# Stores of finished rows and loads of residual rows emitted when they are due, and a shorter assumed trip through DRAM

## The chip, the cores and the metric

The kernel runs on one core of one Trainium2 chip. The metric is the device time of one execution in microseconds (us); each figure is a median over runs.

## The reference

One transformer block with adaptive layer norm, in 32-bit floats, on x of shape (8, 1024, 512) with a condition vector of 512 for each of the 8 sequences:

```
mod = silu(condition) @ Wada + bada
sh_a, sc_a, gt_a, sh_m, sc_m, gt_m = split(mod, 6)
xm = layernorm(x, g1, be1) * (1 + sc_a) + sh_a
x  = x + gt_a * attention(xm, Wqkv, Wproj, bproj)      # 16 heads of 32, causal
xm = layernorm(x, g2, be2) * (1 + sc_m) + sh_m
h  = gelu(xm @ W1 + b1)                                # 512 -> 2048, exact gelu
x  = x + gt_m * (h @ W2 + b2)
```

## The kernel before

**Blocks.** The 8 sequences are cut into 16 blocks of 512 rows (`blocks`, numbered `n`; `NB` is 16). A block holds four tiles of 128 rows. For each block the kernel makes k, q and v, the attention, the projection with the first residual addition (`project_out`, the step "proj"), the second norm ("mt"), the four steps "u" of the up projection with gelu, and the four parts "d" of the down projection. The products k, q, v and up are done by a Strassen scheme (`strassen`) of seven block products named A11, S2, A12, S1, S3, S4, A22 in the order in which TensorE does them; each takes one 256 KB piece of weights. The down projection uses the same scheme in another order.

**Two streams and a planner.** While one block's attention runs, the dense steps of its neighbours run beside it. The order is made once, when the program is built: dense work is written as Python generators (threads) that yield the keys they need. `now` holds a modelled clock for each engine, `written` and `left` hold the modelled times at which a key is written and free again. `work` advances the thread with the shortest modelled wait, side threads ahead of the main one when waits are equal, and what a thread emits goes at once to the ends of the engines' queues. The engines then run those queues strictly in order. So a modelled time decides only where an instruction stands in its queue; on the chip semaphores decide when it runs. The list of dense steps (`plan`) is fixed; at a border between blocks it reads: rest of "u" and "d" of block n-1, "v" of block n+1, "load_xr" of block n, "proj" of n, "mt" of n, "k" of n+2.

**Banks.** Dense products go to three PSUM banks. A bank is free again when VectorE (DVE) or ScalarE (ACT) has copied or combined it out. Inside `strassen`, A11 is copied out to a partial `p1` (traced as `p_v` for v); S2 is combined with it on DVE (`u_v`); A12 is added into A11's bank, which is copied out as the first quarter of the result and freed; S1 takes the third bank and is combined on DVE; S3 needs a bank again; S4 and A22 come last in a side thread.

**The DMA queue.** All loads and stores in question are issued by SyncE (SP), in order; a DMA whose inputs aren't ready holds all that are queued behind it. The weights come through a ring of nine pieces (`fetch`): a load is emitted when the piece nine places earlier is released. Wproj's four pieces stand in this ring between v's and the next k's.

**Residual rows.** `residual[n]` is a tile `xr` of 1 MB in a pool of one buffer (another pool for block 14). "load_xr" (L1268) issues four loads of 256 KB for block n, which must wait until block n-1's rows have been stored. `store(n, t)` (L1104) issues two stores of 256 KB for a pair of tiles; it is called in the last part of "d" right after `settle` has emitted the additions to these rows, most of them on GpSimd (POOL). Both are emitted at the place of the call.

**The trip through DRAM.** For blocks 2 to 15 the normalized rows are transposed without TensorE (`turn`): four DVE transposes of 32x32 blocks, a store of 1 MB to a DRAM tile (`held_a<-xm_a`, L673), four loads of 256 KB back in another order (`hat_a<-held_a`, L678). After each leg `turn` yields until a key is due that the model puts `HOLDING` = 8000 ns after the emission. Then `modulated` emits, one after the other, the instructions that read the loaded tile: four scalings on ACT (L738) or DVE (L732), and subtractions that make the operands T1 to T4 (L746, L748, L158). They are needed only for a later block's k, q and v.

Of the kernel before, what the change touches and what calls it, by code (L numbers as in the profile page):

```python
# [9 lines left out]
F32 = mybir.dt.float32  # L10
# [12 lines left out]
def kernel(  # L23
# [33 lines left out]
    nc = tc.nc  # L57
    B, T, D = x.shape
    HD = W1.shape[1]
    P = 128  # L60
    hd = D // H
    scale = float(hd) ** -0.5
    TB = 512
    NTT = TB // P
# [11 lines left out]
    kvp = ctx.enter_context(tc.tile_pool(name="kvp", bufs=3))  # L76
    act = ctx.enter_context(tc.tile_pool(name="act", bufs=2))
    xrp = ctx.enter_context(tc.tile_pool(name="xrp", bufs=1))
# [11 lines left out]
    blocks = [(b, h) for b in range(B) for h in range(NHALF)]  # L90
    NB = len(blocks)


    now = {"PE": 0.0, "DVE": 0.0, "ACT": 0.0, "POOL": 0.0}
    written, left = {}, {}
    shape = [None]
    pool_spans = []
    NEVER = float("inf")
# [5 lines left out]
    def due(reads=(), writes=()):  # L104
        t = 0.0
        for k in reads:
            t = max(t, written.get(k, 0.0))
        for k in writes:
            t = max(t, left.get(k, 0.0))
        return t  # L110
# [128 lines left out]
    for w in range(1, NB):  # L239
        n = w - 1  # L240
# [27 lines left out]
    n = NB - 1  # L268
# [76 lines left out]
    def take(count):  # L345
        i = taken[0]
        taken[0] += count
        return list(range(i, taken[0]))
# [18 lines left out]
    rows = tmp.tile([P, TB], F32, tag="y", name="rows")[:n_rows, :P]  # L367
    at, r0 = [], 0
# [85 lines left out]
    def half(i, size):  # L454
        return slice(i * size, (i + 1) * size)
# [200 lines left out]
    def turn(key, rows, xm):  # L656
# [16 lines left out]
        nc.sync.dma_start(held, small_blocks)  # L673
        written["held", key] = now["PE"] + HOLDING
        yield [("held", key)], []
        for m in range(NTT):
            some = held[:, ts(m, D)].rearrange("(a i) d -> i a d", i=Q)
            nc.sync.dma_start(rows[ts(m, Q), :, :], some)  # L678
        written["turned", key] = now["PE"] + HOLDING
        yield [("turned", key)], []  # L680

    HOLDING = 8000
    turns = [0]

    def modulated(key, gain, shift, b, guards):
# [68 lines left out]
    def accumulate(pairs, reads=(), close=True):  # L754
        yield reads, [BANK]
        bank = lin_bank()
        for i, (lhsT, rhs) in enumerate(pairs):
            if i:
                yield [], []
            matmul(banks[bank], lhsT, rhs, i == 0, close and i == len(pairs) - 1, reads, bank)  # L760
        return bank
# [227 lines left out]
        yield [("v moved", n)], []  # L989
        vs[n] = v  # L990

    residual, stored = {}, {}
    y_count, y_keys = [0], {}

    def y_key(kind, new=False):
# [5 lines left out]
    LANDING = 10000  # L1001

    def add_to(xt, other, reads, writes, op=ALU.add):
        either(xt, xt, other, op, [*reads, *writes], writes)

    def project_out(n):
        at = take(NC)
        yield [("attended", n)], []
        attT = qTs[n]
        tiles = [residual[n][:, t, :] for t in range(NTT)]  # L1010
        for t, xt in enumerate(tiles):
            xt_job = lambda t=t, xt=xt: add_to(xt, gate_rows["gba"], [("row", "gba")], [("xr", n, t)])
            pool_jobs.append((xt_job, [("xr", n, t)]))
        last = n == NB - 1
        begun = []

        def begin(t):

            bank = yield from accumulate(
                [(attT[:, c, ts(t, P)], piece(at[c])) for c in range(NC - 1)], [("att", n)], False  # L1020
            )
            begun.append(bank)

        for t, xt in enumerate(tiles):
            if last:
                while len(begun) <= max(t, 1):
                    yield from begin(len(begun))
                bank = begun[t]
                yield [("att", n, t)], []
                matmul(  # L1030
                    banks[bank], attT[:, NC - 1, ts(t, P)], piece(at[NC - 1]), False, True,
                    [("att", n, t)], bank,
                )
            else:
                bank = yield from accumulate(
                    [(attT[:, c, ts(t, P)], piece(at[c])) for c in range(NC)], [("att", n)]
                )
            y = tmp.tile([P, D], F32, tag="y", name=f"y_{n}_{t}", bufs=2)
            ky = y_key("proj", True)
            combine_out(y, bank, banks[bank], gate_rows["ga"], [("row", "ga")], [ky], ALU.mult)  # L1040
            if last:
                run_pool_jobs(True)
                nc.vector.tensor_tensor(xt, xt, y, ALU.add)
                note("DVE", 700, [ky, ("xr", n, t)], [("xr", n, t)], port=True)
                following = normalize_tile(xt, f"m{n}", t, ("xr", n, t))
                if t > 0:
                    pending()
                pending = following
            else:
                add_to(xt, y, [ky], [("xr", n, t)])  # L1050
        if last:
            pending()
        release(*at)
        run_pool_jobs(True)
        if not last:
            normalize(residual[n], f"m{n}", [("xr", n, t) for t in range(NTT)])
# [35 lines left out]
    def settle(n, f, t, y, ky):  # L1092
# [4 lines left out]
        add_to(y, gate, [("row", "gm")], [ky], ALU.mult)  # L1097
        add_to(residual[n][:, half(t, 2), c], y, [ky], keys)

    def store(n, t):  # L1100
        b, h = blocks[n]
        for i in (2 * t, 2 * t + 1):
            r0 = h * TB + i * P
            nc.sync.dma_start(out[b, r0 : r0 + P, :], residual[n][:, i, :])  # L1104
        stored[n + 1] = max(stored.get(n + 1, 0.0), due([("xr", n, 2 * t), ("xr", n, 2 * t + 1)]))

    def down(n, part):

# [136 lines left out]
    def perform(step):  # L1245
        kind = step[0]
        if kind == "mod":
            yield from modulation(step[1])
        elif kind == "norm_columns_a":
            columns_of["a"] = norm_columns("a", 0, 1, O_G1, O_BE1)  # L1250
        elif kind == "gates":
            yield from gates(step[1])
        elif kind == "columns_m":
            columns_of["m"] = norm_columns("m", 3, 4, O_G2, O_BE2)
        elif kind == "load_xa":
            x_pre[step[1]] = load_x(step[1])
            written["x", f"a{step[1]}"] = now["PE"] + 6000
        elif kind == "load_xr":
            n = step[1]
            b, h = blocks[n]  # L1260
            if n == NB - 2:
                xr = kvp.tile([P, NTT, D], F32, tag="kT", name=f"xr_{n}")
            else:
                xr = xrp.tile([P, NTT, D], F32, tag="xr", name=f"xr_{n}")
            residual[n] = xr
            for t in range(NTT):
                r0 = h * TB + t * P
                nc.sync.dma_start(xr[:, t, :], x[b, r0 : r0 + P, :])  # L1268
                landed = max(now["PE"], stored.get(n, 0.0)) + LANDING + 700 * t
                written["xr", n, t] = landed  # L1270
        elif kind == "norm_a":
            key = f"a{step[1]}"
            normalize(x_pre.pop(step[1]), key, [("x", key)] * NTT)
        elif kind == "at":
            n = step[1]
            guards = [("m used", n - 3)] if n > 2 else [("v done", 0)] if n == 2 else []
            start(modulated(f"a{n}", *columns_of["a"], blocks[n][0], guards))
        elif kind == "beside":
            start(perform(step[1]))
        elif kind == "sums":  # L1280
            sum_weights(step[1:])
        elif kind == "mt":
            n = step[1]
            guards = [("v done", n + 1)]
            start(modulated(f"m{n}", *columns_of["m"], blocks[n][0], guards))
        elif kind == "k":
            if step[1] != 3:
                yield [("free for k", step[1])], []
            yield from project_T(step, kTs, kvp, "kT", lambda: None)
        elif kind == "q":  # L1290
            yield from project_T(step, qTs, act, "qT", lambda: projected.add(step[1]))
        elif kind == "v":
            yield from project_v(step)
        elif kind == "preps":
            prepared[0] = [preparation(), 0.0]
            written["prepared up"] = written["prepared"] = NEVER
        elif kind == "rows":
            gate_broadcasts(*step[1:])
        elif kind == "proj":
            yield from project_out(step[1])  # L1300
        elif kind == "u":
            yield from up(step)
        elif kind == "d":
            yield from down(*step[1:])
# [19 lines left out]
    def start(it):  # L1324
        thread = [it, None]
        sides.append(thread)
        advance(thread)
# [509 lines left out]
    for n in range(NB):  # L1837
        written["attended", n] = NEVER
        written["v done", n] = NEVER
        written["m used", n] = NEVER  # L1840
        if n > 1:
            written["free for v", n] = NEVER
        if n > 2:
            written["free for k", n] = NEVER
# [70 lines left out]
```

## Time and profile before

| | us |
|---|---|
| median of 3 runs | 3562.32 (3561.42 to 3562.63) |
| profiled execution, its own time | 3568.64 |
| span in that profile | 3566.9 |
| TensorE (PE) busy in it | 3490.9 |
| VectorE (DVE) busy | 2181.1 |
| GpSimd (POOL) busy | 2081.8 |
| ScalarE (ACT) busy | 1186.3 |

The granted TensorE clock was 0.995 over the span. The 2 us between the span and the profiled execution's own time lie outside the first and the last instruction. "SPq" marks an instruction of the DMA queue of SyncE; the name after an arrow in a wait is what ended the wait. A timeline row gives the start, the length, the engine, the line, the operation, the tiles, the number of merged instructions and, in brackets, the idle time before it and who ended it.

### The profile page before, as it was taken

What the parts mean: (1) busy time and instruction counts of PE and PEld (TensorE: products, weight loads), DVE (VectorE), ACT (ScalarE), POOL (GpSimd) and SP (SyncE); (2) the same over time, 40 slices, a digit from 0 to 9 for tenths busy, and PEclk for the clock granted to TensorE, in tenths of its full rate; (3) what the DMA queues carried; (4) which work ended last, traced back from release to release, by engine and by line L of the source; (5) the groups of instructions that cost most, each with busy time, mean ns of one, the idle gap of its engine ahead of it and who ended that gap; (6) DMA issues with size and microseconds to landing.
All of it is one profiled execution on the core that took longest, in us unless ns stands there. A gap on an engine that the chain in (4) does not pass through costs nothing.

```text
span 3566.9 us, 120690 instructions
## 1 busy us (share of the span) xinstructions
PE 3490.9 (98%) x54621; PEld 1741.5 (49%) x54621; DVE 2181.1 (61%) x2395; ACT 1186.3 (33%) x1229; POOL 2081.8 (58%) x2247
## 2 busy tenths in 40 slices
PE   8999999999999999999999999999999999999999
PEld 4444445444554545445454454544545445454445
DVE  6776575665746557365574665746666466665663
ACT  2334333352323514234241442323423134231521
POOL 3667746675456754577536675366762667526660
PEclk9999999999999999999999999999999999999999
DMA  6753434435453344533445334453344533434334
GB/s 201 241 179 93 141 102 127 124 108 155 113 150 107 104 154 117 158 100 101 146 121 148 105 102 146 120 151 103 103 140 126 152 103 105 143 108 142 92 111 137
DMA packets 318259, 461.77 MB, mean 129 GB/s; under 512 B 27052, under 2 KB 177388, under 8 KB 315700
## 3 DMA queue, kind: packets, MB, share of 16 engines
q1 hardware_dynamic: 317632, 454.03, 43.4%
q8 instruction: 430, 7.05, 0.8%
q14 instruction: 81, 0.66, 0.1%
q10 hardware_dynamic: 116, 0.03, 0.0%
HBM read 408.80 MB, written 43.06 MB: 127 GB/s over the span
## 4 chain that ended last, share of the span: by engine, by line
PE 88%; DMA 4%; POOL 3%; DVE 3%; ACT 1%; issue 1%; SPq 1%; ACTq 0%; DVEq 0%; POOLq 0%
PE bank L202 60%; PE sc L1517 8%; PE po L1650 7%; PE st L1610 7%; PE st L1598 3%; DMA w<-in_L_cond_Wproj_dram 2%; PE bank L1671 2%; POOL pT L1740 1%; DMA hat_a<-held_a 1%; PE bank L728 1%; DVE mx L1534 1%; POOL hT L161 1%; PE bank L1572 0%; DVE sc L1531 0%; DMA w<-in_L_cond_Wada_dram 0%
## 5 line engine op out<-in xcount | busy, mean ns | idle before, releaser
L1740 POOL TENSOR_TENSOR pT<-pT,pT 128x256 f32<-128x256 f32 (+3 forms) x1254 | 1213.2, 1003 | 336.1 <-PE po L1650 183.4
L1622 ACT ACTIVATE pT<-st 128x2048 f32<-128x2048 f32 x288 | 541.0, 1878 | 1115.0 <-PE st L1610 1032.9
L202 PE MATMUL bank<-w,hT 128*32 128x256 f32 x14336 | 813.7, 380 | 0.2 <-POOL pT L1627 0.2
L1534 DVE TENSOR_REDUCE mx<-sc 128x4 f32<-128x2048 f32 (+3 forms) x384 | 666.0, 1755 | 216.2 <-PE sc L1517 210.0
L202 PEld LDWEIGHTS bank<-w,hT 128*32 128x32 f32 x14336 | 451.6, 110 | 367.6 <-issue 82.5
L202 PE MATMUL bank<-xm_m,w 128*32 128x256 f32 x8192 | 498.4, 380 | 0.0
L202 PE MATMUL bank<-t_m,w 128*32 128x256 f32 x6144 | 383.2, 380 | 0.1
L202 PEld LDWEIGHTS bank<-xm_m,w 128*32 128x32 f32 x8192 | 256.0, 110 | 222.2 <-issue 55.5
L1627 POOL TENSOR_SCALAR_AFFINE_SELECT pT<-pT 128x512 f32<-128x512 f32 x256 | 169.0, 678 | 332.4 <-ACT pT L1622 332.2
L1517 PE MATMUL sc<-kT,qT 32*128 32x512 f32 (+3 forms) x3072 | 329.1, 520 | 2.0 <-DVE mx L1534 1.7
L1531 DVE TENSOR_TENSOR sc<-sc,mask 128x1024 f32<-128x1024 f32 (+1 forms) x160 | 162.8, 1018 | 273.5 <-PE sc L1517 187.3
L1650 PE MATMUL po<-pT,v 128*32 128x512 f32 (+3 forms) x3048 | 303.1, 493 | 2.0 <-POOL pT L1627 2.0
L1610 PE MATMUL st<-qT,kT 32*128 32x512 f32 (+3 forms) x3072 | 300.6, 487 | 0.0
L202 PEld LDWEIGHTS bank<-t_m,w 128*32 128x32 f32 x6144 | 189.4, 110 | 180.7 <-issue 57.5
L202 PE MATMUL bank<-w,qT 128*32 128x512 f32 x2048 | 244.7, 606 | 21.2 <-DMA w<-in_L_cond_Wproj_dram 19.7
L1689 DVE RECIPROCAL rec<-rec 128x128 f32<-128x128 f32 x256 | 224.5, 919 | 33.2 <-ACT rec L1680 33.2
L202 PE MATMUL bank<-xm_a,w 128*32 128x256 f32 x3968 | 244.6, 380 | 0.0
L1517 PEld LDWEIGHTS sc<-kT,qT 32*128 32x128 f32 x3072 | 129.3, 183 | 172.8 <-ACT pT L1622 63.9
L202 PE MATMUL bank<-t_a,w 128*32 128x256 f32 x2944 | 190.9, 382 | 0.4 <-ACT xm_m L738 0.4
L193 DVE TENSOR_TENSOR hT<-bank,u_u 128x512 f32<-128x512 f32 x192 | 129.3, 685 | 101.2 <-PE bank L202 99.9
L1064 ACT ACTIVATE hT<-hT,cols 128x512 f32<-128x512 f32 x256 | 164.5, 711 | 55.3 <-DVE hT L193 54.7
L202 PEld LDWEIGHTS bank<-xm_a,w 128*32 128x32 f32 x3968 | 123.5, 110 | 106.5 <-issue 30.8
(216 smaller groups left out, 3396.6 us busy)
## 6 DMA issues: line engine op xcount, KB each, us to landing
w<-in_L_cond_W_dram SPq DMA_DIRECT2D x384, 256.0 KB
w<-kept_up_S SPq DMA_DIRECT2D x256, 256.0 KB
w<-kept_down_S SPq DMA_DIRECT2D x256, 256.0 KB
w<-kept_qkv_S SPq DMA_DIRECT2D x180, 256.0 KB
w<-in_L_cond_Wqkv_dram SPq DMA_DIRECT2D x147, 256.0 KB
hat_a<-in_x_dram SPq DMA_DIRECT2D x64, 256.0 KB
w<-in_L_cond_Wproj_dram SPq DMA_DIRECT2D x64, 256.0 KB
xr<-in_x_dram SPq DMA_DIRECT2D x64, 256.0 KB
```

The costliest lines, as they stand in the source:

```text
L193: nc.vector.tensor_tensor(out, src, other, op)
L202: nc.tensor.matmul(ps[r, :], columns, rhs, start=start, stop=stop, skip_group_check=True)
L1064: nc.scalar.activation(hT[:, i, :], hT[:, i, :], AF.Gelu, bias=cols[:, O_B1 + f : O_B1 + f + 1])
L1517: nc.tensor.matmul(sc[:, j, c0 : c0 + w], qTs[n][r, gg, ts(qt, P)], keys_of(n, kh)[r, gg, :w], start=True, stop=True, skip_group_check=True,)
L1531: nc.vector.tensor_tensor(place, place, shape_of.to_broadcast(place.shape), ALU.add)
L1534: nc.vector.tensor_reduce(maxima[n, gg][:, kh, qt, :], sc[:, :, c0 : c0 + w], axis=AX.X, op=ALU.max)
L1610: nc.tensor.matmul(st[:, j, c0 : c0 + w], kT[r, gg, ts(k % NTT, P)], qT[r, gg, TB - w :], start=False, stop=True, skip_group_check=True,)
L1622: nc.scalar.activation(pT[:, :, :used], st[:, :, :used], AF.Exp, scale=scale)
L1627: nc.gpsimd.affine_select(diagonal, diagonal, pattern=[[0, HPG], [1, P]], compare_op=ALU.is_ge, fill=0.0, base=0, channel_multiplier=-1,)
L1650: nc.tensor.matmul(po[r, TB - w :], v[:, k % NTT, g * P + j * hd : g * P + (j + 1) * hd], pT[:, j, c0 : c0 + w], start=(k == 0), stop=last ...
L1689: nc.vector.reciprocal(some, some)
L1740: nc.gpsimd.tensor_tensor(into, into, pT[:, j, c0 : c0 + w], ALU.add)
```

## The change

`store` no longer issues its DMA. It starts a side thread that yields until the additions to the pair of tiles are due by the model, and then emits one DMA of 512 KB in place of two of 256 KB. When both pairs of a block are emitted, the key "stored" of that block is set 3000 ns later (`STORING`). "load_xr" starts a side thread `load_xr(n)`, which yields until "stored" of the block that used the buffer before is due (block 14, in the other pool, waits for nothing; block 15 waits for block 13), and then emits two loads of 512 KB in place of four of 256 KB. The rows are modelled as landed 5000 ns after this plus 700 ns for each tile, where they were modelled at 10000 ns (`LANDING`) plus 700 ns after the later of the emission and the additions. `project_out` now also yields until the loads have been emitted (key "xr begun"). `HOLDING`, the modelled length of each leg of the trip through DRAM, goes from 8000 to 5000 ns.

```diff
--- before.py
+++ after.py
@@ -679,7 +679,7 @@
         written["turned", key] = now["PE"] + HOLDING
         yield [("turned", key)], []
 
-    HOLDING = 8000
+    HOLDING = 5000
     turns = [0]
 
     def modulated(key, gain, shift, b, guards):
@@ -989,7 +989,7 @@
         yield [("v moved", n)], []
         vs[n] = v
 
-    residual, stored = {}, {}
+    residual = {}
     y_count, y_keys = [0], {}
 
     def y_key(kind, new=False):
@@ -1005,7 +1005,7 @@
 
     def project_out(n):
         at = take(NC)
-        yield [("attended", n)], []
+        yield [("attended", n), ("xr begun", n)], []
         attT = qTs[n]
         tiles = [residual[n][:, t, :] for t in range(NTT)]
         for t, xt in enumerate(tiles):
@@ -1097,12 +1097,43 @@
         add_to(y, gate, [("row", "gm")], [ky], ALU.mult)
         add_to(residual[n][:, half(t, 2), c], y, [ky], keys)
 
+    unstored = {}
+
     def store(n, t):
+        unstored.setdefault(n, 2)
+
+        def when_added():
+            b, h = blocks[n]
+            keys = [("xr", n, 2 * t), ("xr", n, 2 * t + 1)]
+            yield keys, []
+            rows = out[b, h * TB + 2 * t * P : h * TB + (2 * t + 2) * P, :]
+            nc.sync.dma_start(rows.rearrange("(t p) d -> p t d", p=P), residual[n][:, half(t, 2), :])
+            unstored[n] -= 1
+            if unstored[n] == 0:
+                written["stored", n] = now["PE"] + STORING
+
+        start(when_added())
+
+    STORING = 3000
+
+    def load_xr(n):
+        before = n - 2 if n == NB - 1 else n - 1
+        if before >= 0 and n != NB - 2:
+            yield [("stored", before)], []
         b, h = blocks[n]
-        for i in (2 * t, 2 * t + 1):
-            r0 = h * TB + i * P
-            nc.sync.dma_start(out[b, r0 : r0 + P, :], residual[n][:, i, :])
-        stored[n + 1] = max(stored.get(n + 1, 0.0), due([("xr", n, 2 * t), ("xr", n, 2 * t + 1)]))
+        if n == NB - 2:
+            xr = kvp.tile([P, NTT, D], F32, tag="kT", name=f"xr_{n}")
+        else:
+            xr = xrp.tile([P, NTT, D], F32, tag="xr", name=f"xr_{n}")
+        residual[n] = xr
+        for t in range(2):
+            rows = x[b, h * TB + 2 * t * P : h * TB + (2 * t + 2) * P, :]
+            nc.sync.dma_start(xr[:, half(t, 2), :], rows.rearrange("(t p) d -> p t d", p=P))
+        for t in range(NTT):
+            written["xr", n, t] = now["PE"] + LOADING + 700 * t
+        written["xr begun", n] = 0.0
+
+    LOADING = 5000
 
     def down(n, part):
 
@@ -1256,18 +1287,8 @@
             x_pre[step[1]] = load_x(step[1])
             written["x", f"a{step[1]}"] = now["PE"] + 6000
         elif kind == "load_xr":
-            n = step[1]
-            b, h = blocks[n]
-            if n == NB - 2:
-                xr = kvp.tile([P, NTT, D], F32, tag="kT", name=f"xr_{n}")
-            else:
-                xr = xrp.tile([P, NTT, D], F32, tag="xr", name=f"xr_{n}")
-            residual[n] = xr
-            for t in range(NTT):
-                r0 = h * TB + t * P
-                nc.sync.dma_start(xr[:, t, :], x[b, r0 : r0 + P, :])
-                landed = max(now["PE"], stored.get(n, 0.0)) + LANDING + 700 * t
-                written["xr", n, t] = landed
+            written["xr begun", step[1]] = NEVER
+            start(load_xr(step[1]))
         elif kind == "norm_a":
             key = f"a{step[1]}"
             normalize(x_pre.pop(step[1]), key, [("x", key)] * NTT)
@@ -1838,6 +1859,7 @@
         written["attended", n] = NEVER
         written["v done", n] = NEVER
         written["m used", n] = NEVER
+        written["stored", n] = NEVER
         if n > 1:
             written["free for v", n] = NEVER
         if n > 2:
```

## The prediction

> **What bounds the kernel now.** I read the page first, then TensorE's waits, then the DMA queue's own waits, then the timeline of one border between blocks, engine by engine.
>
> ```profile
> span 3566.9 us, 120690 instructions
> PE 3490.9 (98%) x54621; PEld 1741.5 (49%) x54621; DVE 2181.1 (61%) x2395; ACT 1186.3 (33%) x1229; POOL 2081.8 (58%) x2247
> ...
> PE 88%; DMA 4%; POOL 3%; DVE 3%; ACT 1%; issue 1%; SPq 1%; ACTq 0%; DVEq 0%; POOLq 0%
> ```
>
> TensorE is busy for 3490.9 of 3566.9 us. The change adds and removes no matmul, so all that it can save lies in the other 76 us; what it can cost is new idle time of TensorE. TensorE's waits say which of the 76 us lie near the change:
>
> ```profile
> PE bank L202 <- DMA w<-in_L_cond_Wproj_dram: 19.7, 14, 3.1
> ...
> PE bank L202 <- DVE v L193: 5.2, 3, 2.1
> ...
> PE bank L202 <- ACT xm_a L738: 1.3, 1, 1.3
> ```
>
> Columns: total us, times, longest. TensorE waits 19.7 us for Wproj's pieces, at the projection that begins each block border. The other two rows are at the same places (a combination of v, or a scaling of a tile back from DRAM, came late). Together 26.2 us: this is the most that I let the change win. The queue in which Wproj's loads stand waits too:
>
> ```profile
> SPq L1104 <- POOL xr L161: 80.5, 23, 9.0
> ...
> SPq L1104 <- DVE xr L158: 24.8, 3, 11.2
> ...
> SPq L1268 <- DMA out_dram<-xr: 11.0, 10, 2.3
> ```
>
> SP stands for 105 us at stores whose additions aren't done, and 11 us at residual loads whose buffer isn't stored yet. One border in order of time, first SP:
>
> ```profile
> 2149.78 0.38 SPq L673 DMA_DIRECT2D held_a<-xm_a  x1
> 2151.08 0.32 SPq L340 DMA_DIRECT2D w<-kept_qkv_S  x1
> 2155.89 1.22 SPq L1104 DMA_DIRECT2D out_dram<-xr  x2
> ...
> 2158.18 0.89 SPq L342 DMA_DIRECT2D w<-in_L_cond_Wproj_dram  x2
> 2161.44 0.82 SPq L1104 DMA_DIRECT2D out_dram<-xr  x2
> 2162.31 3.08 SPq L678 DMA_DIRECT2D hat_a<-held_a  x4
> 2165.49 0.85 SPq L342 DMA_DIRECT2D w<-in_L_cond_Wproj_dram  x2
> ...
> 2168.43 3.73 SPq L1268 DMA_DIRECT2D xr<-in_x_dram  x4
> ```
>
> After the weight load at 2151.08 nothing is issued until the first store at 2155.89; the second pair goes at 2161.44, and the way back from DRAM and the last two Wproj pieces stand behind it. TensorE meanwhile:
>
> ```profile
> 2157.74 1.91 PE L202 MATMUL bank<-w,xm_a 128*32 128x256 f32 x32
> 2159.47 1.91 PE L202 MATMUL bank<-w,t_a 128*32 128x256 f32 x32
> 2161.19 3.64 PE L202 MATMUL bank<-w,xm_a 128*32 128x256 f32 x64
> 2164.65 1.91 PE L202 MATMUL bank<-w,t_a 128*32 128x256 f32 x32
> ...
> 2168.10 1.90 PE L202 MATMUL bank<-w,qT 128*32 128x512 f32 x16
> 2171.79 1.92 PE L202 MATMUL bank<-w,qT 128*32 128x512 f32 x16 [1.79 <-DMA w<-in_L_cond_Wproj_dram]
> 2175.69 3.47 PE L202 MATMUL bank<-w,t_a 128*32 128x256 f32 x32 [1.98 <-DVE v L193]
> ```
>
> The rows are v's A11, S2, A12 with S1, S3; then the projection (w,qT), which runs out of weights and waits 1.79 us, then 1.98 us for DVE. ACT and DVE at the same place:
>
> ```profile
> 2159.76 0.59 ACT L188 COPY p_v<-bank 128x512 f32<-128x512 f32 x1 [13.30 <-PE bank L202]
> 2163.17 0.59 ACT L188 COPY v<-bank 128x512 f32<-128x512 f32 x1 [2.82 <-PE bank L202]
> 2171.36 2.22 ACT L738 ACTIVATE xm_a<-hat_a,shifta,gaina 128x512 f32<-128x512 f32 x3 [7.61 <-DMA hat_a<-held_a]
> ...
> 2161.51 0.69 DVE L193 TENSOR_TENSOR u_v<-bank,p_v 128x512 f32<-128x512 f32 x1 [2.83 <-PE bank L202]
> 2164.95 0.69 DVE L193 TENSOR_TENSOR u_v<-bank,u_v 128x512 f32<-128x512 f32 x1 [2.75 <-PE bank L202]
> 2171.36 0.55 DVE L732 TENSOR_SCALAR xm_a<-hat_a,gaina,shifta 128x512 f32<-128x512 f32 x1 [5.72 <-DMA hat_a<-held_a]
> ```
>
> Both engines stand at the scalings that read the tile back from DRAM. These stand in the queues right behind S1's combination (2164.95), when the model is 16 us past the store at 2149.78 (2165.8): model and chip agree, and only the trip is longer than modelled.
>
> **Part one: stores and residual loads.** The store is emitted when its additions are due, so SP no longer stands at 2151 to 2155.9 and before 2161.4. Weight loads then go when TensorE releases a piece, one each 1.72 us (2159.47 to 2161.19), and Wproj's last piece with the release of A12's, at about 2164.6, where it went near 2166. The projection reads that piece for the first time about 2.5 us after it begins at 2168.10. The traffic of the border (1 MB out, 1 MB back, 1 MB stored, 1 MB of residual rows) also gets spread. I take the 26.2 us as gone: the Wproj waits by the earlier issue, the other two because the blocking scalings move away from there (part two). The gain is bounded by 26.2 above and by 0 below. The residual loads follow 3 us after the second store, which is emitted once the addition behind the store of 2161.44 is done: 2164.4. Main ends its part of v with S3 at 2166.4, so "xr begun" holds nobody by 2 us. If that cover goes, the whole main thread (projection, k, q) is queued behind it, at one us for each us. SP issues half as many stores and residual loads, of twice the size; it had time to spare, and the bytes are the same. The earlier additions to xr (5 for 10 us in the model) are work of POOL and DVE, off the path.
>
> **Part two: 5 for 8 us.** The loads back are now emitted 5 us after the store out, the scalings 10 us after it, where they were emitted at 16. When does the data come? The first trip, with no residual store in the way, and one of the last:
>
> ```profile
> 129.23 1.46 SPq L673 DMA_DIRECT2D held_a<-xm_a  x1
> ...
> 134.78 3.43 SPq L678 DMA_DIRECT2D hat_a<-held_a  x4
> ...
> 144.49 2.21 ACT L738 ACTIVATE xm_a<-hat_a,shifta,gaina 128x512 f32<-128x512 f32 x3
> ...
> 3039.27 0.41 SPq L673 DMA_DIRECT2D held_a<-xm_a  x1
> ...
> 3044.94 2.91 SPq L678 DMA_DIRECT2D hat_a<-held_a  x4
> ```
>
> The way out takes 5.55 and 5.67 us or less, the way back 9.71 at most (134.78 to 144.49, where ACT came from other work) and 9.05 (2162.31 to 2171.36). So I put the tile's landing 14.6 to 15.3 us after the store out (call that moment H), while ACT and DVE will stand at it from about H+10.3 (the model moves in steps of 0.43 us). That wait of 4 to 5 us is no longer than today's; but it falls at v's beginning and not at its end. In this border A11 ends at H+9.9 and its copy gets ahead of the scalings. S2's combination (2161.51 is H+11.7) and the copy that frees A12's bank (H+13.4) come behind them. ACT frees that bank after three scalings and the copy, 2.22 + 0.59 = 2.8 us after the tile lands, at H+17.4 to H+18.1. S3 wants a bank at 2164.65, H+14.87. All three banks are taken, so TensorE waits 2.5 to 3.2 us, with nothing else queued. I count six such borders (v begins 8.0 us after H): 6 x 2.85 = 17.1 us.
>
> In three others v begins 9.7 us after H:
>
> ```profile
> 1706.27 0.38 SPq L673 DMA_DIRECT2D held_a<-xm_a  x1
> ...
> 1717.97 0.59 ACT L188 COPY p_v<-bank 128x512 f32<-128x512 f32 x1 [14.59 <-PE bank L202]
> ...
> 1719.40 3.64 PE L202 MATMUL bank<-w,xm_a 128*32 128x256 f32 x64
> ```
>
> Here A11's copy itself (H+11.7) stands behind the scalings. A12 needs it at 1719.40, H+13.1, and gets it at H+17.4 to H+18.1: 4.3 to 5.0 us, three times, 14.0 us. One border lies between these (v at H+11.0): A12 waits for it from H+14.5, 3.2 us. Four trips are left (two at the start, two where the late store had pushed H back): the scalings meet other work of ACT and DVE there, between 0 and 4 us each, and 1 us each is my estimate: 4 us. Sum 38.3 us. It is bounded below by 0 (the tile comes early enough) and above by 59 us (in the six, too, A11's copy falls behind: A12 waits from H+11.4 to H+17.8, 6.4 us each, 38.4 + 14.0 + 3.2 + 4).
>
> **The sum.** 3568.64 us of the profiled execution - 26.2 + 38.3 = 3580.7. The runs shown have a median of 3562.32, 6.3 lower: 3574.4, forecast 3574.
>
> **Rivals.**
> *Faster: the trip gets shorter once the queue is clear.* If the way back took as little as the way out, 5.6 us, the tile would be there at H+11.2 and S3's bank free at H+14.0, before it is wanted; the three borders would lose 0.9 us each. It decides from a trip of 12 us on. For it: the backlog of stores and loads that stands around hat_a at 2161.44 to 2168.43 goes. Against it: the trip at 129.23 had no residual store beside it and took up to 15.3. Time: 3562.3 - 26.2 + 3 = 3539; halfway, 3551. [...]
>
> *No difference.* The two parts cancel to within 7 us, as with a trip of 13.5 us: the six lose 1.5, the three 3.2, the one 1.8, the four 4 in all; 24 against 26. Time 3560.
>
> *Much slower: A11's copy falls behind the scalings in all ten borders.* The margin is only some 0.4 us (H+10.3 against H+9.9). Time 3562.3 - 26.2 + 59 = 3595.
>
> *It doesn't do what it says.* If the model has the additions done too early, the stores are emitted early and SP stands as today; then part one is lost and part two stays: above 3590. Against it: model and chip agreed at 2165.
>
> **How the numbers follow.** About 0.2% (7 us) is what a measurement can tell from no change. Chances: forecast 0.49, faster 0.26, no difference 0.15, the two slower rivals 0.10. Near the forecast the order of all that follows shifts as well, so its own range is 3567 to 3585 and I leave a twentieth of it inside the 7 us. That makes faster 0.26, same 0.20, slower 0.54. The range 3545 to 3591 leaves out the far half of the faster rival and most of the much slower one.
>
> **What would show it.** SP's waits at stores nearly gone; hat_a issued 5 to 6 us after held_a; Wproj gone from TensorE's waits. In their place TensorE waits at v for `p_v` or `v` on ACT, or for `u_v` on DVE, 2.5 to 5 us in most borders, and DVE's and ACT's waits for hat_a move ahead of u_v. Wrong would be: TensorE without a wait inside v (then 3540), or Wproj still late.

## The result, and the profile after

The changed kernel takes 3618.28 us (median; 3610.07 to 3620.9), beside 3562.48 us (3561.42 to 3575.09) for the kernel before: a ratio of 1.0144, interval 1.0117 to 1.0172. It is slower, as forecast (3574), but by 56 us by the medians (51 by the ratio) where 12 were forecast, and past the upper end of the range (3591). The profiled execution took 3618.11 us; that of the kernel before was 6 us over its median, so the views below show 49.5 of the 56 us.

The page of the kernel after, its span, busy times and chain:

```profile
span 3616.4 us, 120606 instructions
PE 3514.0 (97%) x54621; PEld 1743.9 (48%) x54621; DVE 2153.9 (60%) x2366; ACT 1190.7 (33%) x1236; POOL 2093.2 (58%) x2269
PE 83%; DMA 5%; DVE 5%; POOL 4%; ACT 1%; issue 1%; SPq 1%; ACTq 0%; DVEq 0%; POOLq 0%
```

The span is 49.5 us longer. TensorE's idle time grew from 76.0 to 102.4 us, by 26.4. But its busy time grew too, by 23.1 us, with the same 54621 matmuls: idle time is only about half of the loss. TensorE's waits, of the kernel after (total us, times, longest):

```profile
PE bank L202 <- ACT p_v L188: 15.6, 4, 4.3
PE bank L202 <- ACT v L188: 14.5, 6, 2.9
PE po L1671 <- POOL pT L1648: 10.4, 6, 2.0
...
PE bank L202 <- DMA w<-in_L_cond_Wproj_dram: 4.5, 3, 1.9
...
PE bank L202 <- DVE v L193: 1.6, 1, 1.6
```

The first two rows are the forecast waits inside v, in all ten borders: four for A11's copy `p_v`, six for the copy that frees A12's bank. Wproj is down from 19.7 to 4.5 us and `v` on DVE from 5.2 to 1.6; the wait for a scaling, 1.3 us before, has no row in this list for the dense products. The third row is new in size: there the attention's products wait for POOL, 2.0 us in all before, 10.4 now. The DMA queue's own waits after:

```profile
SPq L1110 <- POOL xr L161: 12.3, 10, 3.0
...
SPq L1131 <- DMA out_dram<-xr: 6.2, 2, 3.6
...
SPq L1110 <- DVE xr L158: 5.3, 3, 3.0
```

SP stands at these stores for 17.6 us in place of 105.3 (the last block has its own, which the change leaves as they were). The border that the prediction showed lies 41.4 us later in the kernel after. Its timeline there, first SP, then TensorE, ACT and DVE:

```profile
2191.16 0.68 SPq L673 DMA_DIRECT2D held_a<-xm_a  x1
2196.73 2.86 SPq L678 DMA_DIRECT2D hat_a<-held_a  x4
2199.63 0.43 SPq L342 DMA_DIRECT2D w<-in_L_cond_Wproj_dram  x1
2200.16 0.40 SPq L1110 DMA_DIRECT2D out_dram<-xr  x1
2200.66 1.42 SPq L342 DMA_DIRECT2D w<-in_L_cond_Wproj_dram  x2
2202.80 0.40 SPq L1110 DMA_DIRECT2D out_dram<-xr  x1
2203.29 0.95 SPq L342 DMA_DIRECT2D w<-in_L_cond_Wproj_dram  x1
2211.72 0.90 SPq L1131 DMA_DIRECT2D xr<-in_x_dram  x2
```

```profile
2199.12 1.91 PE L202 MATMUL bank<-w,xm_a 128*32 128x256 f32 x32
2202.57 3.64 PE L202 MATMUL bank<-w,xm_a 128*32 128x256 f32 x64
2208.26 2.99 PE L202 MATMUL bank<-w,t_a 128*32 128x256 f32 x32 [2.06 <-ACT v L188]
2211.00 1.74 PE L202 MATMUL bank<-w,qT 128*32 128x512 f32 x8
```

```profile
2201.14 0.59 ACT L188 COPY p_v<-bank 128x512 f32<-128x512 f32 x1 [13.30 <-PE bank L202]
2205.51 2.23 ACT L738 ACTIVATE xm_a<-hat_a,shifta,gaina 128x512 f32<-128x512 f32 x3 [3.79 <-DMA w<-in_L_cond_Wproj_dram]
2207.64 0.56 ACT L188 COPY v<-bank 128x512 f32<-128x512 f32 x1
...
2205.52 0.55 DVE L732 TENSOR_SCALAR xm_a<-hat_a,gaina,shifta 128x512 f32<-128x512 f32 x1 [5.46 <-DMA w<-in_L_cond_Wproj_dram]
```

With H = 2191.16: `hat_a` is issued at H+5.6, all four Wproj pieces are issued by H+13.1, and the projection (w,qT) starts without a wait. A11's copy is ahead of the scalings (H+10.0). ACT and DVE then stand at the scalings until the tile lands, at H+14.35 (the profile names Wproj's load there; I take it for `hat_a`, the loaded tile that the scalings read). The copy that frees A12's bank comes behind three scalings, and S3 waits 2.06 us for it. In a border where v begins later, the kernel after has it the other way round:

```profile
1746.80 0.38 SPq L673 DMA_DIRECT2D held_a<-xm_a  x1
...
1763.61 3.66 PE L202 MATMUL bank<-w,xm_a 128*32 128x256 f32 x64 [3.49 <-ACT p_v L188]
...
1760.87 2.22 ACT L738 ACTIVATE xm_a<-hat_a,shifta,gaina 128x512 f32<-128x512 f32 x3 [16.95 <-DMA w<-in_L_cond_Wqkv_dram]
1763.00 0.56 ACT L188 COPY p_v<-bank 128x512 f32<-128x512 f32 x1
```

Here `p_v` itself stands behind the scalings (tile at H+14.07), and A12 waits 3.49 us.

What the 23.1 us of longer busy time are is seen in two views. First, one stretch of the kernel after by the windows of its clock (columns: window, its length, busy us and instructions of PE, PEld, DVE, ACT, POOL, the granted clock, DMA share, GB/s):

```profile
864.15:867.56 3.41, 2.05 (x40) 0.96 (x32) 1.24 (x2) 2.04 (x3) 0.00 (x0) 1.00 1.07 367
867.56:870.98 3.42, 0.44 (x8) 0.29 (x12) 2.45 (x4) 0.77 (x2) 2.44 (x2) 1.00 0.48 180
870.98:874.39 3.41, 3.41 (x36) 1.74 (x32) 0.23 (x1) 0.52 (x1) 1.84 (x2) 0.50 0.00 0
874.39:877.80 3.41, 3.41 (x68) 2.08 (x64) 0.81 (x2) 0.07 (x1) 0.00 (x0) 1.00 0.79 247
```

The wait for `p_v` at this border crosses two windows. TensorE is idle for 2.98 us of the second, and the third runs at half clock: 36 matmuls in a window in which the next has 68. A window of 3.41 us at clock 0.50 costs up to half of its length, 1.7 us, and is shown as busy (3.41 us here). Counted over the clock records (half of the time that stands at half clock), the kernel after loses 27.9 us to this and the kernel before 16.2; the mean granted clocks of 0.992 and 0.995 say the same (0.008 x 3616 = 29, 0.005 x 3567 = 18). That is 11.6 of the 23.1 us.

Second, the row sums of the attention, a group of TensorE instructions, after:

```profile
L1692 PE MATMUL bank<-pT,ones 128*32 128x512 f32 (+3 forms) x536 | 79.1, 583 | 0.0
```

In the kernel before the same 536 matmuls were busy for 71.5 us. These 7.6 us are most of the remaining 11.5; what the other 3.9 are is not shown. They are matmuls over sums that POOL makes just ahead of them, so I took them for waiting, one by one, and shown as busy meanwhile; a place below, under the residual rows, shows it.

### The profile page after: what moved, and what is told of

Same layout as the page of the kernel before. It is cut to its first block, busy times and chain, and to the rows that moved or that the text cites. A ratio compares the mean times of both kernels' runs of the same rounds, so it can differ in the third digit from the quotient of the medians.

```text
span 3616.4 us, 120606 instructions
## 1 busy us (share of the span) xinstructions
PE 3514.0 (97%) x54621; PEld 1743.9 (48%) x54621; DVE 2153.9 (60%) x2366; ACT 1190.7 (33%) x1236; POOL 2093.2 (58%) x2269
## 4 chain that ended last, share of the span: by engine, by line
PE 83%; DMA 5%; DVE 5%; POOL 4%; ACT 1%; issue 1%; SPq 1%; ACTq 0%; DVEq 0%; POOLq 0%
PE bank L202 57%; PE sc L1538 8%; PE po L1671 6%; PE st L1631 6%; PE st L1619 2%; POOL pT L1761 2%; PE bank L1692 2%; DVE mx L1555 2%; DMA held_a<-xm_a 1%; DMA xr<-in_x_dram 1%; DMA w<-in_L_cond_Wproj_dram 1%; PE bank L728 1%; DMA hat_a<-held_a 1%; ACT xm_a L738 1%; POOL hT L161 1%
## 5 line engine op out<-in xcount | busy, mean ns | idle before, releaser
L1671 PE MATMUL po<-pT,v 128*32 128x512 f32 (+3 forms) x3048 | 303.1, 493 | 13.0 <-POOL pT L1648 10.4
```

Source lines behind the costliest of these rows:

```text
L1671: nc.tensor.matmul(po[r, TB - w :], v[:, k % NTT, g * P + j * hd : g * P + (j + 1) * hd], pT[:, j, c0 : c0 + w], start=(k == 0), stop=last ...
```

## The experiments

My theory: the loss comes from the place of the scalings in ACT's and DVE's queues, ahead of v's copies; the stores are a gain by themselves. The rivals: the stores or the traffic cost the time; or the shorter trip does by something other than that place.

| kernel | us (median) | before beside it | ratio (95%) |
|---|---|---|---|
| stores part, LOADING 5000 | 3556.12 | 3566.99 | 0.9971 (0.9962 to 0.9981) |
| trip alone | 3654.52 | 3566.99 | 1.0249 (1.0228 to 1.0269) |
| late return | 3549.50 | 3566.99 | 0.9953 (0.9937 to 0.9970) |
| after, later rows | 3599.13 | 3566.99 | 1.0089 (1.0070 to 1.0108) |
| late return, later rows | 3531.33 | 3563.65 | 0.9903 (0.9887 to 0.9920) |
| the same again | 3530.14 | 3566.67 | 0.9897 (0.9879 to 0.9915) |
| return leg 7000 | 3554.16 | 3563.65 | 0.9972 (0.9960 to 0.9983) |
| copy 5 times | 3572.48 | 3563.65 | 1.0021 (1.0011 to 1.0030) |
| copy 8 times | 3621.14 | 3563.65 | 1.0157 (1.0142 to 1.0172) |
| stores part, later rows | 3538.53 | 3565.92 | 0.9926 (0.9901 to 0.9950) |
| additions shared with DVE | 3548.90 | 3565.92 | 0.9953 (0.9936 to 0.9971) |
| bias additions later | 3542.33 | 3566.67 | 0.9929 (0.9911 to 0.9947) |

**The two parts by themselves.** The stores part is the kernel after with the old length of a leg:

```diff
- HOLDING = 5000
+ HOLDING = 8000
```

> The kernel after with HOLDING back at 8000: the change's stores and residual loads alone. Theory A (the loss is made by the scalings that now stand inside v, by the waits that they give TensorE and the half clock behind these waits): about 3542 us, 3532 to 3552, since the waits for Wproj go and nothing takes their place; TensorE without waits for p_v and v on ACT inside v. Theory B (the loss is made by the new order of stores, residual loads and projection: the projection waits for "xr begun", POOL waits for rows): 3595 to 3620, little less than after.

Measured 3556.12, faster by 11 us: TensorE's waits are as theory A has them, but the gain is less than its range, by 4 us (the rows due at 5 us take it back, as shown below). The trip alone is the kernel before with the new length:

```diff
- HOLDING = 8000
+ HOLDING = 5000
```

> The kernel before with HOLDING at 5000: the shorter trip alone, stores as before. Theory A: 3595 to 3625; TensorE waits inside v for ACT in ten borders, 2 to 5 us each, and the half clock follows some of them. Theory B: 3555 to 3572, as before.

Measured 3654.52, slower by 87.5 and 30 us past theory A's range. TensorE's waits of this kernel:

```profile
PE bank L202 <- ACT v L188: 34.5, 6, 7.0
PE bank L202 <- ACT p_v L188: 34.4, 4, 9.9
...
PE bank L202 <- DMA w<-in_L_cond_Wproj_dram: 8.8, 2, 5.2
```

Those are the waits of after in the same ten places, more than twice as long: with the stores still ahead of it in SP's queue (SP stands at them for 105.5 us), the tile comes later (H+17.0 to H+19.6 in the ten borders). The stores part gains and also shortens the harm of the trip. The rival that blames the stores falls.

**The place of the scalings.** One leg stays at 5000 (the loads back go as early as in after), and the scalings are put 11000 after that, where they stood before:

```diff
- written["turned", key] = now["PE"] + HOLDING
+ written["turned", key] = now["PE"] + RETURNING
+ RETURNING = 11000
```

> The kernel after with two constants: the first leg of the trip stays at 5000, the second is 11000, so that the loads back go as early as after and the scalings stand where they stood before. Theory A: 3530 to 3550, at least as good as the stores alone, because the tile (there 14 to 15 us after the store out) is there before the scalings (16 us). Theory B: 3595 to 3620.

Measured 3549.5, 17.5 us faster than before and, by the ratios (1.0144 and 0.9953), 68 faster than after. A timeline row of ACT in this kernel, at the border shown (`held_a` is stored at 2143.52):

```profile
2159.03 2.23 ACT L739 ACTIVATE xm_a<-hat_a,shifta,gaina 128x512 f32<-128x512 f32 x3 [1.54 <-DMA hat_a<-held_a]
```

It stands for 1.54 us, at H+15.5, and v's copies are by then past; the waits of TensorE for `v` have left the list. The store, the loads and the bytes are those of after. So neither the traffic nor the early loads make the loss; the place of the scalings does. A middle place:

```diff
- RETURNING = 11000
+ RETURNING = 7000
```

> Legs of 5000 and 7000: the scalings are emitted 12 us after the store out, the tile is there at 14 to 15 as before. If what counts is where the scalings stand among v's copies, the six borders with v at H+8.0 have no wait (S2's combination, emitted at H+11.4, is ahead of the scalings, so a bank is free for S3), the three at H+9.7 wait under 1 us (A11's copy, emitted at H+11.4, is ahead), the one at H+11.0 still waits 3 us: 3550 to 3560. If it is the length by which ACT and DVE are held that counts, the loss goes down in proportion, 2.5 us of waiting for 4.5: 3575 to 3590.

Measured 3554.16. TensorE's waits there:

```profile
PE bank L202 <- ACT v L188: 7.6, 6, 1.9
```

The time is as expected for the place. The six borders aren't free, though: the 7.6 us are their waits, now at the start of the projection in place of S3. Two us more between the loads and the scalings take away 22.5 of the 30.1 us of waits for ACT, and 61 of the 68 us (1.0144 to 0.9972). More goes than these waits: of the 62.5 us between the two traces, 35.8 are idle time of all kinds, 17.0 half clock (27.9 to 10.8 by the clock records) and 7.5 shorter row sums (79.1 to 71.6). The next two runs ask for the half clock alone.

**What a wait costs.** In the late-return kernel, A11's copy in v is made several times on ACT, so that A12 waits without any transfer, and no scaling is moved:

```diff
  copy_out(p1, a, blocks_of(a), [k1], last=False)
+ if step[0] == "v":
+     for _ in range(4):
+         nc.scalar.copy(p1, blocks_of(a))
```

> The late return with A11's copy in every v made five times in a row on ACT, to the same place: nothing else changes in the order. The copy ends 2.4 us later, so A12 waits about 1.6 us in some 13 borders, 21 us. A clock that is halved only behind long waits: 3565 to 3575, and no more half clock than in the late return (3 windows of 3.4 us). A clock that follows any wait: 3580 and more.

Measured 3572.48. The second kernel has 7 for 4:

> The same with eight copies: they end 4.1 us later, A12 waits about 3.4 us in some 13 borders, 44 us. Waits alone: 3590 to 3598. With a half clock of 3.4 us behind most of them, 1.7 us each, 17 to 22 us more: 3607 to 3618, granted clock 0.990 or less.

Measured 3621.14. TensorE's waits for A11's copy and the clock of the core, first of the copy made 5 times, then of 8 times:

```profile
PE bank L202 <- ACT p_v L188: 23.9, 15, 4.2
...
core 0: 3570.7 us, clock 0.998
```

```profile
PE bank L202 <- ACT p_v L188: 52.9, 16, 6.1
...
core 0: 3619.8 us, clock 0.990
```

The first 22.1 us of waits (23.9, where the late return has 1.8) cost 24 us (the ratios are 0.0068 apart): one for one. The next 29.0 us of waits cost 48.7 us. The 19.7 us beyond the waits come with the half clock: 19 windows in place of 4, at up to 1.7 us each at most 25.6 us, and less where TensorE waits inside such a window. So waits of 1.49 us, as they are in 13 borders, cost their own length; lengthened to 3.35 us, they cost 1.7 us for each us added.

**The residual rows due at 5 or at 10 us.** The stores part also changed when the additions to `xr` are emitted. Three kernels set the modelled landing of the residual rows back to 10 us:

```diff
- LOADING = 5000
+ LOADING = 10000
```

On the kernel after:

> The kernel after with LOADING at 10000 (residual rows modelled to land as late as before). Theory A: 3605 to 3630, the waits inside v are untouched. Theory B: 3570 to 3600, since POOL's 55 us of waiting for rows go.

Measured 3599.13, 19.2 us faster than after. That is in theory B's range and under theory A's: POOL's 55.1 us of waiting for rows go, as B has it, and the waits inside v stay (16.2 and 15.7 us), as A has it. So the rows' due time is a cost of its own, beside the scalings. On the late return:

> The late return (legs of 5000 and 11000) with LOADING at 10000 as well. If the early modelled landing of residual rows is by itself a cost (POOL held by rows that land later, and the order that follows), 3535 to 3545, some 10 us under the late return. If that cost only comes with TensorE's waits inside v (TensorE behind the model, so the rows behind the model too), no difference: 3545 to 3555.

Measured 3531.33: 18 us faster than the late return (the ratios are 0.0050 apart), and 0.97% faster than the kernel before, the best of all, and under both ranges expected. A second run of it:

> Legs of 5000 and 11000 and LOADING at 10000 once more, beside the run above on one chip: 3528 to 3540 if the best version's gain holds.

gave 3530.14. With the trip at 8000, which is the change's first part with its old landing time:

> The kernel after with HOLDING at 8000 and LOADING at 10000: of the change only the late stores, the residual loads behind them and the larger DMAs are left. If the three parts add up as the runs so far say (stores a gain of some 30 us, early rows a loss of 18, the short trip a loss of 68), 3530 to 3542. If the stores gain only what the stores alone showed (11 us), 3548 to 3558.

3538.53, 27 us faster than before, and 17.6 us faster than the stores part with the rows due at 5 us, a third such pair. The row sums say where the 18 us lie, of the late return and then of the late return with later rows:

```profile
L1693 PE MATMUL bank<-pT,ones 128*32 128x512 f32 (+3 forms) x536 | 83.8, 584 | 1.6 <-POOL pT L1762 1.6
```

```profile
L1693 PE MATMUL bank<-pT,ones 128*32 128x512 f32 (+3 forms) x536 | 70.0, 583 | 0.0
```

13.8 us of busy time and 1.6 us of idle time go. The wait of the attention's products for POOL goes as well, from 5.9 us in the late return to 2.0: 19.3 together, beside 18 measured. On the kernel after the same count is 79.1 to 68.9 and 10.4 to 2.0, 18.6 beside 19.2. POOL at one such place, in the late return and then with later rows:

```profile
1509.52 1.28 POOL L161 TENSOR_TENSOR xr<-xr,y 128x512 f32<-128x512 f32 x1 [7.14 <-DMA xr<-in_x_dram]
1510.88 1.29 POOL L161 TENSOR_TENSOR xr<-xr,row_gba 128x512 f32<-128x512 f32 x1
1512.12 5.98 POOL L1762 TENSOR_TENSOR pT<-pT,pT 128x384 f32<-128x384 f32 x8
```

```profile
1502.91 1.28 POOL L161 TENSOR_TENSOR xr<-xr,y 128x512 f32<-128x512 f32 x1 [6.56 <-DMA xr<-in_x_dram]
1504.15 6.00 POOL L1762 TENSOR_TENSOR pT<-pT,pT 128x384 f32<-128x384 f32 x8
```

In both POOL stands about 7 us for the residual rows, which it reads 7.6 and 7.1 us after their first load is issued (1501.89 and 1495.83): modelled were 5 us in the first kernel and 10 in the second. In the first, one more addition (`row_gba`) lies ahead of the attention's sums on POOL, 1.29 us. POOL's next sums and TensorE's row sums over them, in the same order:

```profile
1519.70 3.20 POOL L1762 TENSOR_TENSOR pT<-pT,pT 128x256 f32<-128x256 f32 x4
1520.91 3.09 PE L1693 MATMUL bank<-pT,ones 128*32 128x512 f32 x8 [0.66 <-POOL pT L1762]
```

```profile
1511.30 3.25 POOL L1762 TENSOR_TENSOR pT<-pT,pT 128x256 f32<-128x256 f32 x4
1516.53 1.04 PE L1693 MATMUL bank<-pT,ones 128*32 128x512 f32 x8
```

In the first, TensorE goes at the pace of POOL's sums and its eight row sums take 3.09 us, shown as busy; in the second POOL is done (1514.55) before they begin, and they take 1.04.

**Which additions it is.** Two kernels on the late return. One gives every second addition of `row_gba` to DVE:

```diff
+ if t % 2:
+     nc.vector.tensor_tensor(xt, xt, gate_rows["gba"], ALU.add)
+ else:
+     nc.gpsimd.tensor_tensor(xt, xt, gate_rows["gba"], ALU.add)
```

> The late return with LOADING at 5000, and the additions of the bias row to the residual rows given in turn to DVE and POOL, where the planner gives most of them to POOL. If early rows cost because they put more additions on POOL, which is then late with the sums that TensorE's row sums wait for: 3528 to 3540, as with LOADING at 10000, and TensorE's row sums again short. If they cost because POOL stands at rows that have not landed: 3545 to 3555, no gain.

Measured 3548.9, no gain over the late return (both 0.9953), with the row sums at 84.7 us. The number of these additions on POOL is not the cause. Nor is it POOL's standing at rows that have not landed: that is 59.3 us in all in the late return and 56.9 with later rows. The other leaves them on POOL and emits them 5 us later, and nothing else:

```diff
- pool_jobs.append((xt_job, [("xr", n, t)]))
+ pool_jobs.append((xt_job, [("xr late", n, t)]))
+ written["xr late", n, t] = written["xr", n, t] + 5000
```

> The late return with LOADING at 5000, and only the additions of the bias row to the residual rows emitted 5 us later than the rows are modelled to land. If early rows cost because these additions stand ahead of POOL's sums of weights (1.3 us each, whichever engine has the rest), 3528 to 3540 and TensorE's row sums near 70 us, as with LOADING at 10000. If the cost comes through the planner's clock for POOL (the additions of the projection push it less far), 3545 to 3553 and row sums near 84 us.

Measured 3542.33, between the two expectations: by the ratios some 9 of the 18 us come back (0.9953 to 0.9929, with intervals of about 0.002 to either side). The row sums are still at 81.4 us; the waits for POOL are down to 2.0. So the early place of these additions is a part of the cost. The rest isn't settled: the additions of `y` to the same rows move with the modelled landing too, and so does what the planner gives to POOL after them. An early due time doesn't cost in every order, either: with the return leg of 7000 the rows are due at 5 us, POOL stands at them for 60.0 us and does 59 of the 64 additions of `row_gba` (52 in the late return), and yet the row sums are at 71.6 us.

## Why the prediction went wrong

**The trip's length: right to within 0.6 us.** The tile was there H+14.0 to H+15.2 in the ten borders (forecast 14.6 to 15.3), so the faster rival, which needed H+12, did not come true: `hat_a` issued at 2196.73 was read at 2205.51, 8.8 us later.

**The waits in v: right.** Forecast were 34.3 us in ten borders, 30.1 were measured, at S3 in six (14.5 us, forecast 17.1) and at A12 in four (15.6, forecast 17.2). The rival in which A11's copy falls behind in all ten did not happen. To the four other trips I put down some 7 us (among them the two waits for `pT` on ACT, 4.9 us), where I had put 4.

**The gain of part one: three quarters right.** Of the waits, 20.1 of 26.2 us went. Wproj kept 4.5, `v` on DVE 1.6.

So the idle time comes out at +26.4, where +12.1 was forecast. The gap of 14.3 is 6.1 (waits of part one that stayed) + 3 (other trips) + 8.4 (products waiting for POOL) - 4.2 (v), 13.3, and 1 us spread over the rest. **Two steps failed.**

*"The earlier additions to xr ... are work of POOL and DVE, off the path."* I priced the 5 for 10 us at nothing and named no work that hid it. The runs show 18 to 19 us, in three pairs. It lies in the attention's part of TensorE, which runs beside the border and takes sums from POOL (row sums 79.1 us for 68.9, waits for POOL 10.4 for 2.0): an engine that is 58% busy is not off the path where TensorE takes its results.

*The sum.* It counts each wait at its length. Against the late return, the early scalings cost 68 us by the runs (3531.33 to 3599.13, both with later rows). The spans and PE busy times of these two kernels make 44 us of it idle time; by the clock records 21 more are half clock (26.5 against 5.5 us). The sum had no such term, though the page of before already showed a clock of 0.995.

The parts add up: the stores part with the rows due at 10 us -27 us, the rows due at 5 us in its place +18, the legs of 5000 in place of 8000 +61 (3538.53 to 3599.13), in all +52, beside 56 measured by the medians and 51 by the ratio. (The 68 us count from the late return, which is 7 us better than legs of 8000.) The stores part alone gained as much as I let it win, but that is luck: in the traces 21.0 us of its gain are idle time, and the loss to the half clock, which I hadn't counted, falls from 16.2 to 3.4 us. The sign of the forecast was right because the waits in v outweigh that gain even without the two missing terms.

## What to carry to other kernels

When a modelled time is shortened, look at what is emitted by it: a load may go early (here, with its readers late, at no cost: the late return has 0.9953, the stores part 0.9971), but the engine that came to an instruction reading its result stood there until the data was there, and what it owed to others stood behind it (at the border shown ACT stood for 3.79 us, and S3 waited 2.06 us for the copy behind). Give the issue of a transfer and the place of its readers a time each, and put the readers where the data comes, not where one hopes for it: that alone turned 1.4% slower into 0.5% faster here. Don't price every wait of TensorE at its length: here those of 1.49 us cost their length, and lengthened to 3.35 us they cost 1.7 us for each us added.

## What was not expected of the hardware

I hadn't counted on windows at half clock behind waits of some 2 us: the sum prices each wait at its length. This is counted in the traces of the kernels before and after, cut into the 3.41 us windows of their clock records, without the first 30 and the last 5 us of each; the idle time is what the matmul records leave of a window.

| TensorE idle in a window at clock 1.00 | windows | next window at clock 0.50 |
|---|---|---|
| below 1.8 us | 2033 | 0 |
| 1.8 to 2.0 us | 7 | 4 |
| 2.0 to 2.2 us | 4 | 4 |
| 2.2 to 3.3 us | 12 | 12 |

The border shown above is one of the four windows with 2.0 to 2.2 us. Its wait of 2.06 us lies in one window, and the next is at clock 0.50 (columns as in the windows before):

```profile
2205.61:2209.02 3.41, 1.35 (x28) 0.62 (x24) 2.36 (x4) 2.60 (x4) 0.48 (x1) 1.00 1.05 400
2209.02:2212.44 3.42, 3.42 (x32) 1.38 (x28) 2.16 (x4) 0.00 (x0) 1.30 (x1) 0.50 0.56 201
```

The longer wait of 3.49 us before 1763.61, shown above too, is split by a window's edge: it leaves 1.72 and 1.77 us of idle time in two windows, and the windows behind them are at clock 1.00. So what a wait cost here beyond its length, nothing or up to 1.7 us, depended on how it fell across the windows. These are counts of two traces; where the limit lies in other kernels they don't show.
